# Gate folded into the output projection, input turned through DRAM, and another order in a transformer block with routed experts

## Chip, cores, metric

One core of a Trainium2 chip. The metric is the device time of one execution in microseconds, median of the runs; the profile is of one execution.

## What is computed

Sixteen sequences of 256 tokens, 256 wide, in float32. Per sequence: a layer norm with a shift from the condition, q, k and v for 16 heads of 64, a layer norm of each head's q and k, softmax attention, the output projection and the residual. Then a softmax gate over 8 experts; each expert takes its 512 best tokens, runs a two-layer network on their normalised rows, and adds the weighted result to them.

```python
h = _ln(x, ln1_g, ln1_b) + silu(t) @ W_ada.T + b_ada
q, k, v = split(h @ Wqkv.T); q, k = _ln(q), _ln(k)
o = softmax(q @ k.T / 8) @ v
x = x + o @ Wout.T
tok = x.reshape(4096, 256)
gate = softmax(tok @ Wgate.T)                  # 8 experts
vals, idx = top_k(gate.T, 512)
y = gelu(_ln(tok[idx]) @ fc1s.T + b1s) @ fc2s.T + b2s
tok = tok.at[idx].add(y * vals)
```

## The kernel before

All products are float32 on TensorE (PE), each showing as two records. A sequence `b` has two tiles `t` of 128 tokens and passes four stages.

- `First`: statistics of the input rows `xs` on VectorE (DVE), the root on GpSimd (POOL), `apply` (normalise, DVE, L632), four PE `transposes` into PSUM (`ph`, L656), and `evict` on ScalarE (ACT), which applies gain and bias and leaves `hT`, the input with its channels on the partitions (L664).
- `Group`, six column groups `g` of 512 by two tiles: the product `pm` (L693). Groups 4 and 5 are v, copied by ACT. Groups 0 to 3 are q and k: square, sum, root, scale; then they are turned. For sequence 0 (`DIRECT`) PE turns them (`pq`). For the others DVE turns blocks of 32 x 32 (`kb`, L762), a DMA writes 512 KB to DRAM (`away`, L769), and another reads them back with the blocks in place (`back`, L780); ACT's `affine` follows.
- `Quad` `d`, four heads at a time, in two halves `i`: `scores` (L819, 64 rows of the array each), `maxima` (DVE, L827), `exps` (ACT, L840), the inverse sums, `normalise` (POOL, L851). The probabilities are turned the same way: DVE (`pb`, L861), `away` (L869), `back` into `prT` (L882). The quads in `OFFS` use PE transposes (`pp`, L888) and an ACT copy (L895) instead. `product` (`po`, L907) uses 64 columns of the array each; `evict` leaves `oT`.
- `Tail`, per tile: `project` (16 records `pw` of 256 columns, L933), `residual` on DVE (`tok`), store, the second norm and its store. For the gate PE transposes `tok` (`pg`, L959), ACT copies it (`tokT`, L965), `gate` multiplies it with `wg` (`pl`, L970, in a PSUM tile of tag `po`), and DVE copies 8 columns to `gates` (L976).

When the gates of sequences 0 to 14 are there, `Routing` transposes them (`turn`, L1035) and finds each expert's threshold bit by bit: 30 rounds of a comparison on DVE, a tiny PE product (`count_over`, L1107) and a decision. Sequence 15's last quads and its projections stand between these rounds. Then 16 `Job`s follow (8 experts, two halves each): a list, a gather by GpSimd, two layers (L1293, L1309), and a scatter-add. From job 1 on the order is in plain Python.

The order up to job 0 is written out. Each step is a call `at(place, engine, took, run, needs, makes, tiles)`; `plan.order(PLACES)` sorts the steps by the numbers in the tuple `PLACES`, one for each step, and calls them; each engine then runs its instructions in that order and waits on semaphores. The other arguments of `at` are a planner's costs and act on nothing in the kernel itself:

```python
at(p, "PE", 3.47, a.project, [("oT", b)], [pw], [pw, ("oT", b)], lag=0.22)
...
for k in plan.order(PLACES):
    plan.steps[k][3]()
```

Nearly all transfers are issued by SP, in order, on one queue (q1): one that waits holds back the rest. Pools bound what can be in flight: `mm` 3 PSUM tiles (pm, ph, pw, pg), `sc` 4, `po` 1; `qk` 3, `sq` 2, `pb` 3, `prT` 4, `blocks` 4 in DRAM.

Of the kernel before, what the change touches and what calls it, by code (L numbers as in the profile page):

```python
# [9 lines left out]
F32 = mybir.dt.float32  # L10
I32 = mybir.dt.int32
BF16 = mybir.dt.bfloat16
AF = mybir.ActivationFunctionType
# [51 lines left out]
def kernel(  # L65
# [6 lines left out]
    woutT: bass.AP,  # L72
    wgateT: bass.AP,
# [75 lines left out]
    def make_others():  # L149
# [21 lines left out]
    DIRECT, OFFS = (0,), {(b, d) for b in (0, B - 1) for d in range(HP // 2)} - {(B - 1, 0), (B - 1, 1)}  # L171
# [11 lines left out]
        0, 0, 3.75, 4.52, 3.3, 4.02, 4.42, 7.76, 0.23, 0, 8, 9.39, 23.39, 15.62, 11.2, 13.11,  # L183
        20.2, 18.21, 0, 0, 0, 0, 0, 0, 0, 3.5, 4.21, 5.54, 5.02, 5.73, 6.59, 7.1, 7.76, 10.88,
        12.83, 14.5, 15.29, 17.61, 24.11, 24.82, 14.6, 16.55, 19.6, 20.39, 22.79, 26.35, 27.24,
        12.61, 14.56, 17.01, 17.93, 21.59, 25.9, 26.57, 18.4, 20.35, 22.19, 22.98, 25.11, 26.8,
        27.91, 22.38, 24.33, 29.19, 31.14, 27.46, 29.41, 30.12, 30.98, 32.96, 34.54, 35.93, 30.92,
        32.87, 33.58, 34.37, 36.58, 49.98, 53.03, 35.14, 39.48, 40.19, 43.73, 45.71, 48.98, 49.77,
        37.37, 39.98, 40.79, 41.85, 43.83, 49.5, 51.4, 39.1, 41.05, 47.25, 49.28, 32.65, 34.78,
        36.6, 38.11, 40.83, 41.54, 34.18, 34.97, 39.02, 41.27, 42.03, 37.84, 42.73, 33.67, 35.38,  # L190
        37.56, 40.03, 41.71, 42.52, 35.98, 38.52, 40.94, 42.15, 43.01, 39.76, 45.64, 46.88, 43.75,
        44.99, 45.78, 51.95, 55.85, 56.57, 46.91, 50.44, 52.86, 56.29, 57.06, 51.68, 58.63, 44.77,
        46.31, 47.37, 53.77, 61.53, 62.58, 47.51, 52.07, 54.68, 65.43, 66.15, 53.31, 66.89, 68.13,
        56.73, 58.17, 58.96, 65.08, 73.25, 73.97, 61.18, 63.07, 69.75, 75.42, 76.14, 64.31, 80.95,
        57.76, 59.98, 61.13, 63.26, 75.86, 76.63, 59.38, 60.17, 64.17, 78.03, 78.74, 62.99, 79.93,
        82.15, 65.87, 67.71, 68.62, 72.43, 89.64, 90.45, 67.11, 69.58, 71.52, 88.18, 88.9, 71.25,
        92.4, 78.91, 80.39, 81.19, 88.14, 94.44, 95.25, 84.26, 85.77, 89.05, 90.23, 94.21, 87.01,
        99.51, 101.48, 112.85, 116.83, 117.98, 117.98, 119.21, 119.72, 119.79, 120.23, 125.51,
        126.28, 116.32, 120.15, 122.66, 121.3, 122.16, 123.66, 125.96, 127.43, 132.51, 133.33, 0,
        15.1, 17.17, 27.27, 12.59, 13.3, 24.78, 46.66, 48.33, 50.66, 53.7, 54.41, 55.59, 57.57,  # L200
        58.77, 54.12, 56.07, 56.78, 59.35, 61.78, 63.16, 52.39, 54.34, 55.05, 57.47, 60.58, 62.38,
        63.18, 64.54, 67.74, 69.34, 74.46, 61.97, 64.03, 64.74, 65.99, 68.31, 69.1, 69.9, 71.34,
        74.54, 76.14, 80.34, 59.65, 62.09, 67.91, 70.54, 63.7, 65.65, 66.36, 67.87, 69.85, 70.64,
        69.79, 71.74, 72.45, 73.34, 75.32, 76.11, 71.52, 73.47, 74.18, 75.22, 77.32, 78.11, 78.91,
        80.27, 83.47, 85.07, 89.39, 73.69, 75.64, 76.72, 77.51, 79.79, 80.99, 81.79, 83.15, 86.35,
        87.95, 93.36, 76.3, 78.25, 82.84, 87.23, 81.82, 83.66, 84.81, 86.32, 87.38, 83.06, 83.85,
        87.23, 88.59, 86.05, 89.39, 90.75, 93.95, 95.55, 104.14, 88.62, 89.86, 90.94, 93.72,
        95.37, 90.46, 91.9, 94.63, 95.98, 93.34, 96.78, 98.14, 101.34, 102.94, 108.93, 114.54,
        93.42, 94.77, 95.74, 103.48, 104.54, 96.59, 101.97, 104.39, 106.35, 103.21, 107.15,
        108.51, 111.73, 113.93, 127.28, 98.49, 99.73, 100.52, 105.3, 109.36, 100.33, 102.93,  # L210
        106.21, 110.57, 104.17, 111.37, 112.73, 116.16, 118.36, 128.3, 129.49, 105.16, 107.56,
        108.71, 114.78, 117.83, 106.96, 107.75, 112.05, 116.22, 111.78, 122.3, 124.9, 128.1,
        129.97, 139.32, 106.18, 108.76, 111.12, 112.96, 114.39, 108.16, 110.16, 113.87, 115,
        112.55, 115.8, 117.16, 120.7, 122.9, 138.3, 140.41, 109.95, 112.72, 115.03, 120.22,
        125.07, 111.95, 113.58, 119.31, 129.55, 119.04, 130.35, 131.97, 135.17, 136.77, 142.08,
        121.74, 123.27, 124.06, 126.71, 130.68, 123.87, 125.02, 127.62, 128.94, 126.44, 131.48,
        133.17, 136.77, 138.77, 143.1, 145.7, 159.6, 163.6, 164.95, 164.75, 166, 166.55, 173.78,
        174.91, 176.32, 177.22, 163.07, 167.2, 168.65, 168.35, 170.41, 172.99, 176.77, 179.56,
        180.45, 181.22, 0, 26.23, 27.18, 28.97, 25.71, 26.42, 27.6, 78.47, 79.23, 84.72, 86.73,
        87.99, 89.96, 91.94, 92.73, 86.45, 88.4, 89.2, 91.84, 94.17, 97.19, 90.67, 92.86, 93.57,  # L220
        95.54, 97.8, 99, 99.8, 101.16, 104.36, 106.14, 112.08, 95.03, 96.98, 98.4, 99.19, 101.17,
        101.96, 102.94, 104.94, 108.14, 109.74, 115.99, 96.76, 103.89, 107.05, 109.67, 100.53,
        104.88, 105.75, 107.12, 109.97, 115.61, 102.41, 104.38, 105.15, 109, 111.18, 121.15,
        110.97, 113.08, 113.79, 115.69, 118.44, 119.54, 120.34, 121.7, 124.9, 126.5, 132.75,
        120.01, 121.96, 122.67, 123.46, 125.68, 126.61, 127.41, 128.77, 131.97, 134.37, 139.02,
        123.63, 126.94, 129.17, 131.31, 122.76, 127.74, 128.53, 132.16, 133.49, 124.47, 125.98,
        133.07, 134.7, 131.89, 138.37, 140.77, 143.97, 145.57, 155.83, 126.26, 128.34, 130.35,
        138.22, 139.83, 131.29, 135.85, 139.13, 140.44, 137.09, 141.24, 142.6, 145.8, 147.57,
        154.81, 156.92, 131.49, 132.73, 133.75, 136.4, 148.24, 134.1, 134.89, 137.31, 147.02,
        136.13, 149.04, 150.99, 154.95, 157.79, 171.89, 140.19, 142.03, 142.82, 145.91, 156.57,  # L230
        141.43, 143.78, 146.82, 153.56, 145.64, 157.37, 159.79, 162.99, 164.59, 172.91, 175.21,
        141.21, 143.23, 144.74, 154.31, 160.52, 145.04, 149.04, 151.52, 159.91, 150.28, 161.39,
        163.39, 167.05, 168.99, 185.54, 149.31, 150.55, 151.34, 158.04, 161.73, 154.17, 154.96,
        158.95, 162.34, 157.18, 164.59, 166.59, 169.79, 171.39, 184.52, 188.07, 150.33, 152.35,
        157.41, 160.92, 170.74, 154.77, 158.37, 160.01, 169.8, 159.74, 174.92, 177.12, 180.72,
        182.72, 190.02, 156.7, 157.94, 162.28, 165.51, 175.49, 159.14, 161.32, 166.42, 171.95,
        165.2, 176.29, 178.32, 182.68, 185.92, 191.04, 192.13, 198.43, 202.27, 204.54, 203.47,
        204.66, 207, 215.16, 215.88, 216.4, 217.76, 206.68, 210.37, 212.02, 212.16, 213.19,
        216.86, 213.06, 216.18, 222.5, 223.22, 0, 28.45, 29.46, 48.11, 26.75, 27.94, 48.44,
        131.05, 131.8, 133.11, 137.31, 138.12, 140.04, 142.63, 143.83, 134.84, 136.81, 137.52,  # L240
        141.92, 144.44, 146.41, 136.57, 138.52, 139.23, 143.8, 145.81, 147.63, 148.43, 149.79,
        152.99, 154.59, 159.33, 145.85, 147.8, 148.85, 149.64, 151.75, 152.95, 154.59, 156.59,
        159.79, 161.39, 165.59, 143.97, 146.19, 153.08, 155.92, 147.58, 150, 151.15, 152.43,
        155.97, 162.99, 151.2, 153.3, 155.37, 156.16, 158.54, 166.59, 157.72, 160.33, 161.13,
        161.92, 164.6, 165.39, 166.19, 167.79, 171.39, 173.39, 179.86, 166.54, 168.49, 169.2,
        169.99, 172.56, 173.76, 174.56, 175.92, 179.12, 180.72, 184.92, 168.27, 170.22, 174.59,
        176.65, 170, 173.16, 173.95, 178.17, 179.23, 171.35, 172.14, 179.08, 180.61, 177.71,
        182.32, 184.72, 187.92, 189.52, 195.52, 171.02, 174.37, 178.1, 180.11, 181.38, 176.1,
        177.14, 181.02, 182.59, 179.84, 184.92, 187.92, 191.12, 192.72, 212.04, 214.1, 182.63,
        185.36, 186.15, 193.17, 194.4, 184.76, 187.11, 192.26, 193.79, 190.79, 196.32, 198.54,  # L250
        205.4, 207.74, 219.75, 183.65, 190.19, 190.98, 194.08, 195.61, 187.17, 189.06, 194.99,
        196.22, 192.22, 197.02, 199.74, 202.94, 204.54, 218.73, 221.32, 196.54, 198.38, 199.53,
        202.56, 203.88, 197.78, 198.57, 201.65, 203.27, 201.38, 205.04, 206.54, 214.9, 217.74,
# [1392 lines left out]
```

## Time and profile before

| | |
|---|---|
| median of 3 runs | 1074.48 us (1072.66 to 1075.8) |
| profiled execution | 1075.44 us, its span 1073.7 us |
| busy in the span | PE 1039.4, DVE 822.4, POOL 617.5, ACT 588.9 us |
| mean granted PE clock | 0.986 |
| q1: packets, MB, share of 16 DMA engines | 156992, 235.44, 64.7% |

The span runs from the first to the last instruction. Records of PE overlap, so a row's mean length (609 ns for a pm record) is more than the distance between starts, which is what a record costs a full PE. Rows name a line, an engine, output and inputs, shape, count, busy time and mean, then the idle time before them and what ended it. Windows give each engine's busy time in a stretch, the granted clock and the share of the DMA engines.

### The profile page before, as it was taken

Reading aid. Unit: us, or ns where it says so; the run is one execution under the profiler, and the core shown is the slowest. Engines: PE = TensorE matmul, PEld = TensorE weight load, DVE = VectorE, ACT = ScalarE, POOL = GpSimd, SP = SyncE. Lnnn points to the kernel's source line nnn. Section 1 sums busy time; section 2 is a strip of 40 time slices with the busy share of each in tenths; the row PEclk is TensorE's granted clock in tenths of the full one; section 3 lists DMA queues with packets and bytes.
Section 4 is the critical chain, followed back from the end, with each engine's and each line's share of the span. In section 5 each row is a group of like instructions: output and inputs, shape, how many; then the busy total and the mean of one; then the engine's idle time right before and its main releaser. Section 6 shows DMA issues by size and latency. Waiting matters only on the chain. (4 is left out here: it accounts for less than half of the span.)

```text
span 1073.7 us, 17767 instructions
## 1 busy us (share of the span) xinstructions
PE 1039.4 (97%) x5547; PEld 681.8 (64%) x5547; DVE 822.4 (77%) x2281; ACT 588.9 (55%) x1646; POOL 617.5 (58%) x997
## 2 busy tenths in 40 slices
PE   7899999999999999999999999999789999999996
PEld 4455656555554655656565565666468888888885
DVE  6667888989888898798888888888667588655440
ACT  1577676666666666575766667675503422333331
POOL 3666776778667686766767676674401433333332
PEclk7999999999999999999999999999999999999998
DMA  6014889888987898888888898889430656665661
GB/s 217 1 60 157 279 289 319 293 294 277 309 281 262 282 317 303 294 291 271 280 296 304 280 306 282 290 315 312 147 103 21 196 146 180 196 184 155 185 204 20
DMA packets 165005, 246.85 MB, mean 230 GB/s; under 512 B 9520, under 2 KB 135728, under 8 KB 164912
## 3 DMA queue, kind: packets, MB, share of 16 engines
q1 hardware_dynamic: 156992, 235.44, 64.7%
q0 software_dynamic: 6144, 8.39, 4.3%
q10 hardware_dynamic: 1776, 1.90, 0.5%
q8 instruction: 44, 0.72, 0.3%
q14 instruction: 49, 0.40, 0.1%
HBM read 140.84 MB, written 104.86 MB: 229 GB/s over the span
## 5 line engine op out<-in xcount | busy, mean ns | idle before, releaser
L693 PE MATMUL pm<-wq,hT 128*128 128x512 f32 x768 | 362.0, 609 | 7.0 <-DVE qk L730 4.2
L851 POOL TENSOR_SCALAR pr<-pr,sums 128x256 f32<-128x256 f32 x512 | 238.2, 485 | 97.2 <-DVE sums L847 90.8
L840 ACT ACTIVATE pr<-sc,nmax 128x256 f32<-128x256 f32 x512 | 237.8, 480 | 101.5 <-DVE nmax L827 77.6
L693 PEld LDWEIGHTS pm<-wq,hT 128*128 128x128 f32 x768 | 138.2, 191 | 162.5 <-issue 137.2
L103 POOL TENSOR_TENSOR ss<-ss,neghalf 128x8 f32<-128x8 f32 x128 | 210.7, 1646 | 10.7
L827 DVE TENSOR_REDUCE nmax<-sc 128x2 f32<-128x512 f32 x256 | 165.8, 676 | 14.3 <-PE sc L819 13.6
L861 DVE STREAM_TRANSPOSE pb<-pr 128x512 f32<-128x512 f32 x232 | 154.2, 687 | 7.4 <-POOL pr L851 6.9
L819 PE MATMUL sc<-kT,qT 64*128 64x256 f32 x1024 | 135.2, 394 | 0.0
L907 PE MATMUL po<-prT,v 128*64 128x256 f32 x1024 | 128.7, 389 | 2.9 <-DMA prT<-blocks 2.9
L706 ACT ACTIVATE sq<-pm 128x512 f32<-128x512 f32 x128 | 76.7, 604 | 92.0 <-PE pm L693 91.0
L819 PEld LDWEIGHTS sc<-kT,qT 64*128 64x128 f32 x1024 | 91.3, 186 | 46.9 <-issue 28.5
L1326 POOL DMA_INDIRECT out<-y,idx x32 | 51.1, 1597 | 120.1 <-DVE y L1320 66.2
L1293 PE MATMUL ph<-xT,w 128*128 128x256 f32 x512 | 117.6, 383 | 0.0
L1309 PE MATMUL py<-w,hid 128*128 128x256 f32 x512 | 116.3, 380 | 0.0
L933 PE MATMUL pw<-wo,oT 128*128 128x256 f32 x512 | 115.2, 381 | 0.0
L907 PEld LDWEIGHTS po<-prT,v 128*64 128x64 f32 x1024 | 66.8, 137 | 68.7 <-issue 19.3
L933 PEld LDWEIGHTS pw<-wo,oT 128*128 128x128 f32 x512 | 96.3, 190 | 21.0 <-issue 5.8
L840 ACT ACTIVATION_READ_ACCUMULATOR pr<-sc,nmax 128x1 f32 x512 | 108.0, 211 | 0.0
L730 DVE TENSOR_TENSOR qk<-pm,ss 128x512 f32<-128x512 f32 x128 | 89.7, 702 | 22.8 <-POOL ss L103 20.8
L1300 ACT ACTIVATE hid<-ph,vec 128x256 f32<-128x256 f32 x128 | 60.4, 474 | 84.2 <-PE ph L1293 77.2
L1309 PEld LDWEIGHTS py<-w,hid 128*128 128x128 f32 x512 | 95.6, 190 | 12.8
L1293 PEld LDWEIGHTS ph<-xT,w 128*128 128x128 f32 x512 | 95.5, 190 | 12.9
(142 smaller groups left out, 1081.6 us busy)
## 6 DMA issues: line engine op xcount, KB each, us to landing
blocks<-pb SPq DMA_DIRECT2D x116, 512.0 KB
prT<-blocks SPq DMA_DIRECT2D x116, 512.0 KB
kblocks<-kb SPq DMA_DIRECT2D x60, 512.0 KB
w<-in_fc2T SPq DMA_DIRECT2D x16, 1024.0 KB
w<-in_fc1T SPq DMA_DIRECT2D x16, 1024.0 KB
qraw<-kblocks SPq DMA_DIRECT2D x30, 512.0 KB
kT<-kblocks SPq DMA_DIRECT2D x30, 512.0 KB
out<-tok SPq DMA_DIRECT2D x32, 128.0 KB
```

The costliest lines, as they stand in the source:

```text
L103: nc.gpsimd.tensor_tensor(dst, src, neghalf[:, : src.shape[1]], ALU.pow)
L693: nc.tensor.matmul(self.pm, hTs[self.b][:, c, bass.ts(self.t, P)], wq[:, c, bass.ts(self.g, GW)], start=(c == 0), stop=(c == DC - 1),)
L730: engine.tensor_tensor(dst, src.rearrange("p (q e d) -> p q e d", q=QB, e=8), by_head(self.ss[:, 1, :]), ALU.mult,)
L819: nc.tensor.matmul(self.sc[i, j][:, t, :], qTs[self.b][rows, hp, bass.ts(t, P)], keys[rows, hp] if whole else keys[rows, hp // 4, hp % 4], ...
L827: nc.vector.tensor_reduce(self.nmax[i, j], self.sc[i, j], AX.X, ALU.max, negate=True)
L840: nc.scalar.activation(dst, src, AF.Exp, bias=self.nmax[i, j][:, t : t + 1], scale=1.0, accum_out=self.sums[i][:, 0, j, t : t + 1],)
L851: nc.gpsimd.tensor_scalar(self.pr[i, j][:, t, :], self.pr[i, j][:, t, :], self.sums[i][:, 1, j, t : t + 1], 1.0, ALU.mult, ALU.mult,)
L861: nc.vector.transpose(self.pb[i][:, :, :, j].rearrange("p k c t n -> p t k c n"), self.pr[i, j].rearrange("p t (k c m) -> p t k c m", c=TB ...
L907: nc.tensor.matmul(self.po[j * HD : (j + 1) * HD, i, :], vs[self.b][:, c, bass.ts(4 * self.d + 2 * i + j, HD)], prT[:, j, c] if (self.b, s ...
L933: nc.tensor.matmul(self.pw, oTs[self.b][:, hp // 2, self.t, hp % 2, :], wo[:, hp, :], start=(hp == 0), stop=(hp == HP - 1),)
L1293: nc.tensor.matmul(self.ph[f], self.w1[:, c, bass.ts(f, P)], self.xT[:, c, :], start=(c == 0), stop=(c == DC - 1),)
L1309: nc.tensor.matmul(self.py[i], self.hid[:, f, bass.ts(i, P)], self.w2[:, f, :], start=(f == 0), stop=(f == FC - 1),)
```

## The change

- `wo` gets 8 more columns per head pair: Wout transposed times the gate matrix, computed once by `Fold` from a second load of Wout (1 MB). `project` then yields the attention's share of the gate's logits beside the projection; two more products add the share of the input, from `xT`, the input transposed on the host and loaded for each sequence (256 KB). The transposes of `tok`, the copy and the gate's own step go.
- The normalised input of sequences 1 to 15 is turned by DVE and through DRAM (`xblocks`, 256 KB out in 2-KB rows and back in 512-byte pieces), no longer by PE; `apply` moves to GpSimd for them. The buffers are of the tags `qk` and `sq`. Weights and vectors are permuted on the host to match (`quarters`).
- Quads 2 and 3 of sequence 0 leave `OFFS`: they go through DRAM, too.
- `PLACES` is another list, with other costs in the `at` calls.

```diff
-    ... {(B - 1, 0), (B - 1, 1)}
+    ... {(B - 1, 0), (B - 1, 1), (0, 2), (0, 3)}
+    XDIRECT = (0,)
-    PLACES = (0, 0, 3.75, 4.52, 3.3, ...)
+    PLACES = (...)
-        wo = attw.tile([P, HP, D], F32, name="wo")
+        wo = attw.tile([P, HP, D + E], F32, name="wo")
+        def load_xT(b):
+            xTs[b] = seq.tile([P, DC, N], F32, tag="xT", bufs=1, name=f"xT{b}")
+            nc.sync.dma_start(xTs[b], xT[:, b * N : (b + 1) * N].rearrange("(c p) n -> p c n", p=P))
+        class Fold:
+            def load(self):
+                self.w = seq.tile([P, DC, H * HD], F32, tag="oT", bufs=2, name="wout")
+                nc.sync.dma_start(self.w, wout.rearrange("(c p) f -> p c f", p=P))
+            def product(self):
+                self.pf = ps.tile([P, HP, E], F32, tag="mm", bufs=3, name="pf")
+                for hp in range(HP):
+                    for c in range(DC):
+                        nc.tensor.matmul(self.pf[:, hp], self.w[:, c, bass.ts(hp, P)], wg[:, c],
+                            start=(c == 0), stop=(c == DC - 1))
+            def evict(self):
+                nc.scalar.copy(wo[:, :, D:], self.pf)
 class First:
+                self.norms[t].apply(dst, nc.vector if self.b in XDIRECT else nc.gpsimd)
+            def turn(self, t):
+                if t == 0:
+                    self.xb = work.tile([P, QB, DC, TB, SQ], F32, tag="qk", bufs=3, name="xb")
+                nc.vector.transpose(...)
+            def away(self):
+                self.blocks = dram.tile([QB, SQ, QB, P], F32, tag="xblocks", bufs=2, name="xblocks")
+                nc.sync.dma_start(...)
+            def back(self):
+                self.raw = work.tile([P, QB, DC, TB, SQ], F32, tag="sq", bufs=2, name="xraw")
+                nc.sync.dma_start(...)
+            def affine(self):
+                for c in range(DC):
+                    nc.scalar.activation(hTs[b][:, c]..., self.raw[:, :, c], AF.Identity, bias=..., scale=...)
 class Tail:
-            def project(self, a=0, b=HP):
+            def project(self):
+                self.pw = ps.tile([P, D + E], F32, tag="mm", bufs=3, name="pw")
                 for hp in range(HP):
                     nc.tensor.matmul(self.pw, oTs[...], wo[:, hp, :], start=(hp == 0), stop=False)
+                for c in range(DC):
+                    nc.tensor.matmul(self.pw[:, D:], xTs[self.b][:, c, bass.ts(self.t, P)], wg[:, c, :],
+                        start=False, stop=(c == DC - 1))
-            def transposes(self): ...
-            def evict(self): ...
-            def gate(self): ...
             def gate_evict(self):
-                nc.vector.tensor_copy(gates[:, self.n, :], self.pl)
+                nc.vector.tensor_copy(gates[:, self.n, :], self.pw[:, D:])
```

## The prediction

> **What bounds the kernel now.** I read the page first (busy shares, slices, queues), then the windows by stage, the order of time on PE around one sequence's end, the waits of PE, and the order of time where the sequences give way to the routing.
>
> From the page: PE is busy nearly throughout, and the DMA slices are the only others near nine.
>
> ```profile
> PE 1039.4 (97%) x5547; PEld 681.8 (64%) x5547; DVE 822.4 (77%) x2281; ACT 588.9 (55%) x1646; POOL 617.5 (58%) x997
> ...
> DMA  6014889888987898888888898889430656665661
> ...
> q1 hardware_dynamic: 156992, 235.44, 64.7%
> ```
>
> The windows (stretch, length, busy time of each engine, granted clock, DMA share, GB/s) split it into stages.
>
> ```profile
> 60.00:100.00 40.00, 40.00 (x187) 21.55 (x187) 28.32 (x50) 30.02 (x81) 28.97 (x46) 1.00 0.34 119
> 100.00:750.00 650.00, 649.62 (x3186) 375.20 (x3183) 562.65 (x1123) 432.59 (x1279) 460.73 (x796) 1.00 0.86 291
> 750.00:821.00 71.00, 58.03 (x441) 44.99 (x440) 51.74 (x261) 21.29 (x63) 17.60 (x37) 0.93 0.32 105
> 821.00:1074.00 253.00, 242.85 (x1548) 212.60 (x1546) 141.39 (x767) 78.43 (x161) 82.15 (x67) 0.99 0.55 156
> ```
>
> From 60 to 750 us PE never rests, so each sequence takes as long as its PE work. The projections of sequences 0 and 13 begin at 120.28 and 717.76, which is 46.0 us a sequence. DVE is at 87% there, POOL at 71%, DMA at 86%. From 750 to 821 the routing's chain between DVE and PE sets the time; from 821 the experts run, which the change doesn't touch. So the question is when the routing's first transpose (L1035) can run.
>
> The order of time on PE (start, length, line, records) gives prices as distances between starts:
>
> ```profile
> 177.61 2.00 PE L819 MATMUL sc<-kT,qT 64*128 64x256 f32 x16
> 179.54 1.95 PE L907 MATMUL po<-prT,v 128*64 128x256 f32 x16
> 181.42 0.44 PE L959 MATMUL pg<-ident,tok 128*128 128x128 f32 x2
> 181.69 0.60 PE L656 MATMUL ph<-ident,xn 128*128 128x128 f32 x4
> 182.13 1.88 PE L693 MATMUL pm<-wq,hT 128*128 128x512 f32 x4
> 183.85 0.51 PE L970 MATMUL pl<-wg,tokT 128*128 128x8 f32 x4
> 184.21 0.42 PE L959 MATMUL pg<-ident,tok 128*128 128x128 f32 x2
> 184.47 3.60 PE L693 MATMUL pm<-wq,hT 128*128 128x512 f32 x8
> ```
>
> The four transposes of the input cost 0.44 us (181.69 to 182.13), the two of tok 0.27 and 0.26, the gate's four records 0.36. Ahead of another full-array product four pm records take 1.72 (182.13 to 183.85); ahead of scores they took 1.81 (175.80 to 177.61), so a change between whole array, half rows (scores) and half columns (products) costs 0.09.
>
> **The change, part by part, to the routing's transpose.** Counts are from PE's order in the two programs, up to that transpose.
> - Input transposes of sequences 1 to 15 go: 15 x 0.44 = -6.6.
> - The tok transposes of 30 tiles go: 30 x 0.26 = -7.8.
> - The gate's two products per tile become two of xT with the same gate weights: 30 x 0.36 out, the same in, 0.
> - The projection gets 264 columns for 256. Its 32 records of sequence 14 run from 743.63 to 750.74, 0.222 each; 8/256 of that, 16 records, 30 tiles: +3.3.
> - The fold is 16 products of the gate's kind (two in 0.36): +2.9. It stands in the head, where PE idles (16.69 of 20 us busy from 20 to 40), so it may cost nothing; I count it.
> - Quads 2 and 3 of sequence 0 go through DRAM, while two of sequence 15's transposing steps move ahead of the routing: 64 transposes become 40, 24 x 0.11 (0.44/4) = -2.6.
> - One more half-quad product stands ahead: +0.9 (1.88 for two).
> - The other order changes array shape 286 times, where the old one did 258: 28 x 0.09 = +2.5. The diff doesn't say this; it takes back a sixth of what the transposes give.
>
> The sum is -6.6 - 7.8 + 3.3 + 2.9 - 2.6 + 0.9 + 2.5 = **-7.4 us** of PE work.
>
> The Trainium skill (TensorEngine Tiling, Key Properties) says that changing the tiling mode drains TensorE, and gives no time. The 0.09 us above is that price here; without it the sum would read -9.9.
>
> Beside the path: DVE loses 30 applies (0.43 each, -13.0) and gains 30 turns of 128x256 (between 0.34, half of L861's 0.69, and 0.69; I take 0.38, +11.4) and 8 turns of sequence 0 (+5.5): 4 us more on an engine with 87 us free in the stage. ACT loses the tokT copies and 8 prT copies (-12.2 - 4.8) and keeps the affine at its size. The applies go to POOL, 30 x 0.485 as L851's: +14.6, ahead of normalisations that wait there; POOL has 189 us free. SP issues some 55 more transfers of 0.3 to 0.5 us. Its new waits matter more: each `back` of the input waits for its write, as L882 does (95.3 us over 53 waits, 1.8 each), and behind it stand the writes of other quads. That is hidden as long as the products come later than their data. The input's own exchange is well covered: between its affine and the first product that reads hT stand three to eleven steps of PE, 3.5 us or more.
>
> DMA is the cover that wears thin. Per sequence three transfers of 0.262 MB come in (input out, input back, xT); 291 GB/s x 46.0 is 13.4 MB now. PE's new period is about 45.5, so 14.2 MB in it is 311 GB/s, a share of 0.86 x 311/291 = 0.92. By packets the input's read is worse: 512 of 512 bytes, which at q1's mean packet (64.7% of 16 x 1073.7 us over 156992, 0.071 us) would take 2.3 us of all engines against 0.8 by bytes. So the share lies between 0.92 and 0.95.
>
> The Trainium skill (DMA: Bandwidth & Descriptors, Bandwidth) puts HBM per core at about 358 GB/s. By that alone there would be 13% left; this trace shows no 650-us stage near it, only 291.
>
> What a late transfer costs shows where DMA is fullest:
>
> ```profile
> PE po L907 <- DMA prT<-blocks: 2.9, 3, 1.1
> ```
> ```profile
> 743.63 7.17 PE L933 MATMUL pw<-wo,oT 128*128 128x256 f32 x32
> ...
> 757.05 1.13 PE L819 MATMUL sc<-kT,qT 64*128 64x256 f32 x8
> ...
> 759.17 1.08 PE L907 MATMUL po<-prT,v 128*64 128x256 f32 x8 [0.98 <-DMA prT<-blocks]
> ...
> 760.18 0.50 PE L1035 MATMUL pgT<-ident,gate_of 128*128 128x128 f32 x2
> ```
>
> All three waits of the trace, 0.95 us each, lie at 759 to 765, after the experts' first weights were queued; one is ahead of the routing's transpose. In the sequence stage there is none. At 0.92 and over I don't expect none: I take three more, +2.9, with bounds of none (0) and one per sequence (14 x 0.95 = 13.3).
>
> After the transpose, the old loop holds both projections of sequence 15, tok's transposes and the gate; the new one has one projection inside and one behind, ahead of the totals. DVE's decisions now wait up to 2.7 us for PE (790.55), once per projection; so it may save 2.7 us or, if the totals wait longer than the round did, cost 1 (PE's 3.7 for a projection less 2.7). I take 0.
>
> So -7.4 + 2.9 = **-4.5 us**. The profiled execution took 1075.44 (span 1073.7 and 1.7 around it) and becomes 1070.9; it was 0.96 over the median of 1074.48, so the median becomes **1070.0**.
>
> **Rivals.**
> 1. *DMA becomes the bound (slower).* Products wait for prT in the sequence stage. One 0.95 us wait per sequence gives -7.4 + 13.3 = +5.9, 1080.4. Eight waits eat the saving; from eleven on it is slower by over 0.3%. For it: 5-us windows from 705 to 750 already show shares of 0.96 to 1.07. Against it: PE rode over them without a wait.
> 2. *The gain is lost at the end (no change).* Ahead of the routing's transpose now stand three products of sequence 15 instead of two, with an expert's 2.2 MB of weights queued before their reads. Three waits more there, with the three above: -7.4 + 2.9 + 2.9 = -1.6, 1072.9.
> 3. *No waits, and a shorter loop (much faster).* -7.4 - 2.7 = -10.1, 1064.4.
>
> **How the numbers follow.** A run of this kernel tells about 0.3% (3.2 us) from no change: faster means under 1071.3, slower over 1077.7. The forecast with its neighbourhood (1066.5 to 1071.3) gets 0.46, rival 3 gets 0.08, rival 2 0.22, rival 1 0.24. Faster 0.54, same 0.22, slower 0.24. The range runs from 1064.0, rival 3, to 1081.0, just past rival 1's price; below it lies 0.05, above it 0.15.
>
> **What would show it.** Right: PE still busy in all of 100 to 750, the projections of sequences 0 and 13 about 45.5 us a sequence apart, no ph rows but sequence 0's, DMA share 0.91 to 0.95, the routing's transpose near 755. Wrong: more than eight waits of PE or its weight loads for prT, qT or kT; a DMA share of 0.97 and up with PE under 640 of 650; or the transpose early but the experts' first product not (then the loop took it). A head that ends later, by the fold or by late keys of sequence 1, would move the first projection past 120.

## The result, and the profile after

| | before | after |
|---|---|---|
| median of 4 runs | 1073.57 us (1071.77 to 1075.8) | 1087.53 us (1084.88 to 1088.7) |
| profiled execution, span | 1075.44, 1073.7 | 1088.7, 1087.0 |
| routing's first transpose on PE | 760.18 | 772.65 |
| from there to the experts' first product | 60.51 | 61.18 |

The ratio of the means is 1.0126 (95%: 1.0097 to 1.0154). The forecast was 1070.0, the range 1064.0 to 1081.0: the change made the kernel slower, by more than any case that I had priced. All but 0.7 of the 13.3 us between the profiled executions lie ahead of the routing's transpose.

The page of the kernel after (busy times; slices; the SP queue):

```profile
PE 1039.5 (96%) x5423; PEld 670.9 (62%) x5423; DVE 822.0 (76%) x2289; ACT 575.8 (53%) x1607; POOL 654.5 (60%) x1027
...
DMA  7028899998899998989898799899403556655661
...
q1 hardware_dynamic: 174384, 252.74, 68.5%
```

The windows of the kernel after, the second cut at the same places as before, the third up to the experts' first product:

```profile
100.00:750.00 650.00, 641.27 (x3038) 356.01 (x3037) 555.39 (x1119) 422.56 (x1245) 485.01 (x810) 1.00 0.90 307
750.00:834.00 84.00, 66.75 (x476) 51.49 (x477) 57.38 (x270) 22.89 (x69) 22.99 (x49) 0.89 0.35 120
```

PE does 124 records fewer in all and is no less busy; in the sequence stage it now rests 8.7 us of 650, where it rested 0.4. The DMA share of that stage is 0.90, under the 0.92 to 0.95 that I gave. POOL is busy 37 us more in all, where I had 14.6. Two rows of GpSimd after show why:

```profile
L927 POOL TENSOR_SCALAR pr<-pr,sums 128x256 f32<-128x256 f32 x512 | 237.4, 485 | 93.4 <-DVE sums L923 82.8 <-PE pm L769 2.6
...
L672 POOL TENSOR_SCALAR xn<-xs,mv,rs 128x256 f32<-128x256 f32 x30 | 37.1, 1241 | 0.9
```

The apply has the shape of the normalisation that I took its price from, and takes 1.241 us for 0.485. What that does shows in the waits of ACT and DVE from 100 to 745 us (total, times, longest), first before, then after:

```profile
ACT pr L840 <- DVE nmax L827: 70.7, 51, 4.6
...
DVE qk L730 <- POOL ss L103: 13.3, 27, 1.4
```
```profile
ACT pr L916 <- DVE nmax L903: 94.4, 60, 4.7
...
DVE qk L806 <- POOL ss L105: 28.2, 32, 2.5
```

And one such place in the order of time after:

```profile
422.32 2.43 POOL L672 TENSOR_SCALAR xn<-xs,mv,rs 128x256 f32<-128x256 f32 x2
...
425.12 1.67 POOL L105 TENSOR_TENSOR ss<-ss,neghalf 128x8 f32<-128x8 f32 x1
...
426.82 0.69 DVE L806 TENSOR_TENSOR qk<-pm,ss 128x512 f32<-128x512 f32 x1 [2.49 <-POOL ss L105]
...
427.56 1.98 PE L769 MATMUL pm<-wq,hT 128*128 128x512 f32 x4 [0.76 <-DVE qk L806]
...
428.02 2.47 DVE L903 TENSOR_REDUCE nmax<-sc 128x2 f32<-128x512 f32 x4
...
429.39 0.47 ACT L916 ACTIVATE pr<-sc,nmax 128x256 f32<-128x256 f32 x1 [1.92 <-DVE nmax L903]
...
431.23 1.10 PE L769 MATMUL pm<-wq,hT 128*128 128x512 f32 x2 [1.69 <-DVE qk L806]
```

Two applies hold the root of q and k's norm back; DVE stands 2.49 us for it, with the maxima behind in its order; ACT stands for the maxima; PE stands twice for `qk`, whose PSUM tile it needs.

The end of the sequences, PE after:

```profile
744.19 1.64 PE L895 MATMUL sc<-kT,qT 64*128 64x256 f32 x10
747.93 1.94 PE L895 MATMUL sc<-kT,qT 64*128 64x256 f32 x6 [2.10 <-DVE pb L937]
750.88 2.08 PE L895 MATMUL sc<-kT,qT 64*128 64x256 f32 x8 [1.01 <-ACT kT L870]
752.89 2.93 PE L983 MATMUL po<-prT,v 128*64 128x256 f32 x16
...
769.56 1.08 PE L983 MATMUL po<-prT,v 128*64 128x256 f32 x8 [1.56 <-DMA prT<-blocks]
```

There is nothing but sequence 15's own chain to do at 746 to 751, and after the waits the granted clock falls: 0.81 from 745 to 750, 0.51 from 750 to 755, and eight score records take 2.08 us for 1.13. The Trainium skill (TensorE: Matmul & The Clock Gate, Part 1) says that the clock goes to half rate after an idle window of about 3.4 us. The 0.51 agrees with the half; the idle time does not, since PE's longest rest here was 2.10 us.

**PE's time up to the routing's transpose**, counted from the starts of its records: *work* is records times their usual distance to the next (medians: pm 0.429, pw 0.216 or, with 264 columns, 0.222, a transpose 0.109, scores 0.1085, products 0.108, fold 0.112, and the gate's four in 0.364); *changes* are what a stretch of one array shape takes on top of that (0.199 for the whole array, 0.104 on its first pm record and 0.094 on its last; 0.196 for scores, 0.150 for products); *rest* is what remains, split at 60 and 700 us. Each row is of one profiled execution, and executions of one kernel differ by up to 7 us (f3: 1074.09 to 1081.1), so differences of a microsecond say little.

| kernel | transpose at | work | changes | rest | head, sequences, end |
|---|---|---|---|---|---|
| before | 760.2 | 688.5 | 47.7 | 24.0 | 20.7, 1.8, 1.5 |
| after | 772.7 | 680.1 | 52.5 | 40.0 | 22.0, 9.4, 8.6 |
| e1, applies on DVE | 767.3 | 680.1 | 52.5 | 34.7 | 20.8, 5.6, 8.3 |
| h1, cheap apply on GpSimd | 767.2 | 680.1 | 52.5 | 34.6 | 20.8, 5.6, 8.1 |
| f4, e1 and the tail moved | 766.7 | 680.1 | 52.9 | 33.6 | 19.7, 5.3, 8.6 |
| g1, f4 and weights later | 763.8 | 680.1 | 52.9 | 30.7 | 21.5, 6.1, 3.2 |
| h3, g1 and xT loaded once | 760.0 | 680.1 | 52.9 | 26.9 | 19.4, 4.4, 3.1 |
| e5, before with the slow apply on GpSimd | 772.2 | 688.5 | 47.7 | 36.0 | 23.7, 10.4, 1.8 |
| h4, before with the cheap apply there | 766.6 | 688.5 | 47.7 | 30.4 | 23.6, 5.3, 1.4 |
| f3, before with spare traffic | 762.0 | 688.5 | 47.7 | 25.8 | 18.8, 3.9, 3.2 |
| g2, before with the fold | 768.8 | 688.4 | 46.5 | 33.9 | 19.6, 9.3, 5.0 |

The change does take PE's time off, 8.37 of work less 4.83 of changes, 3.5 us; the rest grows by 16.0.

### The profile page after: what moved, and what is told of

It is laid out like the page before. It is cut to its first block, busy times and chain, and to the rows that moved or that the text cites. A ratio compares the mean times of both kernels' runs of the same rounds, so it can differ in the third digit from the quotient of the medians.

```text
span 1087.0 us, 17596 instructions
## 1 busy us (share of the span) xinstructions
PE 1039.5 (96%) x5423; PEld 670.9 (62%) x5423; DVE 822.0 (76%) x2289; ACT 575.8 (53%) x1607; POOL 654.5 (60%) x1027
## 5 line engine op out<-in xcount | busy, mean ns | idle before, releaser
L903 DVE TENSOR_REDUCE nmax<-sc 128x2 f32<-128x512 f32 x256 | 164.3, 673 | 16.9 <-PE sc L895 16.5
L937 DVE STREAM_TRANSPOSE pb<-pr 128x512 f32<-128x512 f32 x240 | 157.9, 684 | 9.9 <-POOL pr L927 7.7
L895 PE MATMUL sc<-kT,qT 64*128 64x256 f32 x1024 | 138.3, 399 | 4.1 <-DVE pb L937 2.1
L983 PE MATMUL po<-prT,v 128*64 128x256 f32 x1024 | 132.8, 392 | 3.8 <-DMA prT<-blocks 3.3
L1008 PE MATMUL pw<-wo,oT 128*128 128x264 f32 x512 | 122.4, 393 | 0.0
L786 DVE TENSOR_REDUCE ss<-sq 128x8 f32<-128x512 f32 x128 | 85.4, 668 | 25.2 <-ACT sq L782 24.3
```

Source lines behind the costliest of these rows:

```text
L895: nc.tensor.matmul(self.sc[i, j][:, t, :], qTs[self.b][rows, hp, bass.ts(t, P)], keys[rows, hp] if whole else keys[rows, hp // 4, hp % 4], ...
L903: nc.vector.tensor_reduce(self.nmax[i, j], self.sc[i, j], AX.X, ALU.max, negate=True)
L937: nc.vector.transpose(self.pb[i][:, :, :, j].rearrange("p k c t n -> p t k c n"), self.pr[i, j].rearrange("p t (k c m) -> p t k c m", c=TB ...
L983: nc.tensor.matmul(self.po[j * HD : (j + 1) * HD, i, :], vs[self.b][:, c, bass.ts(4 * self.d + 2 * i + j, HD)], prT[:, j, c] if (self.b, s ...
L1008: nc.tensor.matmul(self.pw, oTs[self.b][:, hp // 2, self.t, hp % 2, :], wo[:, hp, :], start=(hp == 0), stop=False,)
```

## Experiments: the applies

Three theories. 1: the applies on GpSimd hold back the chain root, scale, maxima, exponentials, PE. 2: the fuller DMA delays data. 3: the order itself, with its end stage. Ratios are to the kernel before, run beside each.

**e1**, the changed kernel with the applies on DVE:

```diff
-                self.norms[t].apply(dst, nc.vector if self.b in XDIRECT else nc.gpsimd)
+                self.norms[t].apply(dst, nc.vector)
```

> The changed kernel with one thing undone: the normalisation of the input (xn) of sequences 1 to 15 is applied by DVE, as in the kernel before, not by GpSimd; everything else, the exchange and the order included, as changed. Theory 1 (the 30 applies on GpSimd, 1.24 us each, hold back the roots behind them, and through DVE, the maxima and the exponentials PE): 7 to 10 us less than the changed kernel, 1077 to 1080, idle of DVE for the root's result back from 28 to about 14 us in the sequence stage, routing's transpose at 763 to 766. Theory 2 (the fuller DMA) and theory 3 (the other order itself, with its end stage): within 2 us of the changed kernel, 1086 to 1089.

1081.15 us, ratio 1.0062 (1.0048 to 1.0076): half of the loss, a little less than theory 1 had. DVE's wait for the root went down less than expected:

```profile
DVE qk L806 <- POOL ss L105: 21.5, 29, 2.1
```

**e5**, the kernel before with only the applies moved to GpSimd:

```diff
...
-                self.norms[t].apply(self.xn[t])
+                self.norms[t].apply(self.xn[t], nc.gpsimd if self.b else nc.vector)
```

> The kernel before with one thing of the change alone: the normalisation of the input of sequences 1 to 15 is applied by GpSimd in the old order, nothing else. Theory 1: 30 applies of 1.24 us on GpSimd, 3 to 12 us slower than before, 1077 to 1086, with more idle of DVE for the root's result (13.3 us before in the sequence stage). Theory 2 and theory 3: no change, within 2 us of 1074.

1088.45 us, 1.0137 (1.0122 to 1.0152). In an order that was laid for them on DVE the 30 instructions alone lose as much as the whole change does.

**f1**, the changed kernel, each apply as two instructions:

```diff
...
+                    nc.gpsimd.tensor_scalar(dst, norm.src, norm.mv[:, 0:1], None, ALU.subtract)
+                    nc.gpsimd.tensor_scalar(dst, dst, norm.rs[:, 1:2], None, ALU.mult)
```

> The changed kernel with each apply on GpSimd written as two instructions, a subtraction with one pointer and a multiplication with one pointer, for the one instruction with both that took 1.24 us. If the 1.24 us comes from having two operations in one instruction, each of the two costs about 0.48 as the multiplication of the probabilities does, 0.97 together, GpSimd loses 8 us and theory 1 expects 1 to 3 us less than the changed kernel (the gain of putting the applies back on DVE, 6.4 us for 37 us of GpSimd, in proportion). If each of the two costs 0.6 or more, the price is of the data and not of the form, and the time stays within 1 us or grows. Theories 2 and 3: no change.

A miss: 1102.55 us, 1.0271 (1.0252 to 1.029). Each of the two costs nearly twice what I took:

```profile
L698 POOL TENSOR_SCALAR xn<-xn,rs 128x256 f32<-128x256 f32 x30 | 28.3, 945 | 2.8
L697 POOL TENSOR_SCALAR xn<-xs,mv 128x256 f32<-128x256 f32 x30 | 28.0, 933 | 0.0
```

The same multiplication by a pointer takes 0.479 us at the probabilities, where the code adds a second operation, times 1.0. So the form was at stake, and **g4** looked at five forms by turns (the sequence's number modulo 5 chooses):

```diff
...
+                if form == 0:
+                    ts(dst, src, mu, rs, ALU.subtract, ALU.mult)
+                elif form == 1:
+                    ts(dst, src, rs, nm, ALU.mult, ALU.add)
+                elif form == 2:
+                    ts(dst, src, mu, 1.0, ALU.subtract, ALU.mult)
+                    ts(dst, dst, rs, 1.0, ALU.mult, ALU.mult)
+                elif form == 3:
+                    ts(dst, src, nm, rs, ALU.add, ALU.mult)
+                else:
+                    ts(dst, src, rs, 1.0, ALU.mult, ALU.mult)
+                    ts(dst, dst, nm, 1.0, ALU.add, ALU.mult)
```

> A look at the price of forms: the changed kernel, its apply on GpSimd written in five ways by turns over the sequences, all of which compute the same. (a) subtract pointer, multiply by pointer in one instruction: 1.24 us as measured. (b) multiply by pointer, add pointer: 1.24 if the price is that of two pointers. (c) subtract pointer, times the constant 1.0; then multiply by pointer, times the constant 1.0: 2 x 0.48 if the price is that of the second pointer, 2 x 0.93 if only multiplications are cheap. (d) add pointer, multiply by pointer: as (b). (e) multiply by pointer, times 1.0; add pointer, times 1.0: 0.48 and 0.48 or 0.93. The probabilities' normalisation (multiply by pointer, times the constant 1.0) took 0.48, the single operation with no second one 0.93.

Its rows (1084.93 us, one run):

```profile
L704 POOL TENSOR_SCALAR xn<-xs,mv,rs 128x256 f32<-128x256 f32 x6 | 7.3, 1219 | 0.4
L708 POOL TENSOR_SCALAR xn<-xs,mv 128x256 f32<-128x256 f32 x6 | 6.9, 1148 | 0.2
...
L706 POOL TENSOR_SCALAR xn<-xs,rs,nm 128x256 f32<-128x256 f32 x6 | 3.3, 555 | 0.6
L711 POOL TENSOR_SCALAR xn<-xs,nm,rs 128x256 f32<-128x256 f32 x6 | 3.3, 548 | 0.7
...
L713 POOL TENSOR_SCALAR xn<-xs,rs 128x256 f32<-128x256 f32 x6 | 2.9, 478 | 0.0
L714 POOL TENSOR_SCALAR xn<-xn,nm 128x256 f32<-128x256 f32 x6 | 2.9, 478 | 0.6
```

Neither the second pointer nor addition is dear (0.555, 0.548, 0.478): the subtraction is (1.219, 1.148). Adding the negated mean does the same for less than half.

**h1**, the changed kernel with that form (**h4**: the same in the kernel before):

```diff
...
+                nc.gpsimd.tensor_scalar(nm, norm.mv[:, 0:1], -1.0, 1.0, ALU.mult, ALU.mult)
+                nc.gpsimd.tensor_scalar(dst, norm.src, nm, norm.rs[:, 1:2], ALU.add, ALU.mult)
```

> The changed kernel with one thing changed: the apply on GpSimd adds the negated mean and then multiplies, for subtracting the mean and multiplying (0.55 us in place of 1.22, and a GpSimd instruction of 128x1 of 0.19 for the sign): 22 us of GpSimd for 37. If the loss goes with GpSimd's time, 6.4 x 15/37 = 2.6 us less than the changed kernel, 1084 to 1085.5. If it is the long instruction that holds back the roots behind it, most of the 6.4 us comes back: 1081 to 1083. If the place itself matters (any apply on GpSimd), under 1 us.

1081.89 us, 1.0062 (1.0049 to 1.0074), the ratio of e1. The two waits of the chain fall with it: ACT's for the maxima from 94.4 to 78.8 us, DVE's for the root from 28.2 to 22.1. Together: 0 us of applies on GpSimd give 1.0062, 22.6 us in short instructions 1.0062, 37 us in 1.24-us ones 1.0126, 56 us in pairs of 0.94 1.0271. Within the intervals of e1 and h1, some 1.4 us to each side, the form is all of theory 1's loss in this order, and the place costs nothing.

> The kernel before with the applies of sequences 1 to 15 on GpSimd in the cheap form, old order. The slow form cost 14 us there. In proportion to GpSimd's time (22 of 37 us): 8 us slower, 1081 to 1084. If the long instruction was the trouble: 0 to 4 us slower, 1074 to 1079.

1081.40 us, 1.0049 (1.0036 to 1.0062) for 1.0137: in between. In the old order the place costs something, too; of its 6.4 us more rest 2.9 are in the head, where sequence 1's applies join GpSimd's queue.

## Experiments: the traffic

**e4**, the changed kernel with `xT` loaded once, and **h3**, the same on g1 (below):

```diff
+            if b:
+                xTs[b] = xTs[0]
+                return
             xTs[b] = seq.tile([P, DC, N], F32, tag="xT", bufs=1, name=f"xT{b}")
```

> The changed kernel with the transposed input loaded once, for sequence 0, and used for all 16 sequences (the gate's logits are then of another input: that part of the computation is changed). It takes 15 of the 45 new transfers of 0.26 MB and their issues on SP away. Theory 2: 2 to 4 us less than the changed kernel. Theory 1: 1 us less at most. Theory 3: 0 to 1 us less, through the freer SP queue in the end stage.

1084.15 us, 1.0095 (1.008 to 1.011); 3.4 us less than the changed kernel by the medians, 0.0031 less in the ratio, though the intervals overlap a little.

**f3**, the kernel before with 42 spare transfers:

```diff
...
+                if aways[self.b] in (2, 5, 7):
+                    spare = dram.tile([N, D], F32, tag="spare", bufs=4, name="spare")
+                    nc.sync.dma_start(spare, x[self.b * N : (self.b + 1) * N])
```

> The kernel before, old order, no part of the change, with three spare transfers of 0.26 MB (rows of the input to a scratch buffer in DRAM, read by nobody) issued by SP in each of sequences 1 to 14, 42 in all, 11 MB: the change's own additional traffic without its steps. Theory 2: 3 to 8 us slower than before (the changed kernel lost 3.4 us less with a third of its traffic taken away). Theories 1 and 3: within 1.5 us of 1074.

1077.01 us, 1.0026 (1.0013 to 1.004): 2.7 us, just under theory 2's range.

> The kernel with the moved tail and the weights later (1078.5), with the transposed input loaded once and used for all sequences (the gate's logits are then of another input: that part of the computation is changed). Theory 2: a third of the additional traffic less gives 1.5 to 3 us, 1075.5 to 1077, as 3.4 were gained by the same edit on the changed kernel and 2.7 lost by 11 MB of spare traffic on the kernel before. If that gain was GpSimd's or the end stage's, now gone: within 1 us of 1078.5.

1076.47 us, 1.0008 (0.9999 to 1.0018) for g1's 1.0037: 3 us again, with GpSimd and the end stage out of the way. So loading `xT` for every sequence costs about 3 us. PE itself waits for no transfer in the sequence stage; ACT and DVE do. From 100 to 745 us their waits for transfers come to 4.1 us before, 9.8 after, 16.9 in g1 and 9.1 in h3 (one execution each).

Whether the bytes or SP's queue carry it isn't told apart, since loading `xT` once takes both away. One thing speaks for the queue. `xT` has a single buffer, so SP stands until the projections of the sequence before have read it, 21.2 us in 13 waits of the changed kernel from 100 to 745 us, and whatever comes next on the queue stands behind it, here a read of prT:

```profile
SPq L573 <- PE pw L1013: 21.2, 13, 3.7
```
```profile
406.00 0.37 SPq L958 DMA_DIRECT2D prT<-blocks  x1
410.09 0.38 SPq L573 DMA_DIRECT2D xT<-in_xT  x1
410.57 0.42 SPq L958 DMA_DIRECT2D prT<-blocks  x1
```

The spare transfers of f3 show no such wait, and 11 MB of them cost no more than the 4 MB of `xT`. A second buffer for `xT` was not tried.

## Experiments: the end stage

**f4**, e1 with sequence 13's second projection, its followers and the load of `xT` 14 moved into the idle time:

```diff
+        MOVED = {
+            3278: 721.2, 3279: 727.9, 3286: 727.95, ...
+            3284: 730.2, 3285: 732, 3502: 725.6, ...
+        }
-        for k in plan.order(PLACES):
+        for k in plan.order([MOVED.get(k, p) for k, p in enumerate(PLACES)]):
```

> The changed kernel with the applies back on DVE and one more edit: the second projection of sequence 13, with its followers and the load of sequence 14's transposed input, is moved from among sequence 15's last matrix products to the place where PE idles between the scores of sequence 15 (2.1 and 1.8 us of waits, and 2.5 us more at a lower granted clock after them). Theory 3 (the order of the end stage leaves PE without independent work there): 3 to 6 us less than 1081.2, that is 1075 to 1078. If the idle time comes from a chain that just starts later (transfers, exponentials), nothing is gained: 1080 to 1082.

1080.59 us, 1.006 (1.0046 to 1.0073): no gain. The projections of sequence 14 began at 746.1 for 752.5, but PE lost it all at the next transfer (order of time of PE, then of SP's issues):

```profile
756.14 1.13 PE L895 MATMUL sc<-kT,qT 64*128 64x256 f32 x8
761.21 1.97 PE L983 MATMUL po<-prT,v 128*64 128x256 f32 x8 [3.93 <-DMA prT<-blocks]
```
```profile
747.73 0.44 SPq L1268 DMA_DIRECT2D w<-in_fc2T  x1
748.26 0.89 SPq L1270 DMA_DIRECT2D w<-in_fc1T  x1
...
749.85 3.00 SPq L945 DMA_DIRECT2D blocks<-pb  x2
752.90 6.01 SPq L958 DMA_DIRECT2D prT<-blocks  x2
```

An expert's 2.1 MB of weights stand ahead of the write, and the read's issue waits for that write, 6 us for two.

**g1** is f4 with that load moved behind sequence 15's reads:

```diff
...
+            3916: 743.0,
...
```

> The kernel with the applies on DVE and the moved tail of sequence 13 (1080.6), with one more edit: the first load of an expert's weights (2.1 MB) is issued behind the last reads of sequence 15's probabilities, not ahead of them. In the version before it PE lost its two waits of 2.1 and 1.8 us, but then stood 3.93 us (and 1.5 more at a lower clock) for prT behind those weights. If the weights on the queue are what makes that read late (rival 2 of the prediction): 4 to 5.5 us less, 1075 to 1077, no wait of PE for prT over 1 us ahead of the routing's transpose. If the read is late by its own chain (turns, write, wait of SP): within 1.5 us of 1080.6.

1078.53 us, 1.0037 (1.0023 to 1.0051): 2 us by medians, half of what I expected, but the mechanism is there: the wait is 0.58, the clock 1.00 from 740 to 764, the end's rest 3.2 for 8.6.

```profile
760.46 1.08 PE L983 MATMUL po<-prT,v 128*64 128x256 f32 x8 [0.58 <-DMA prT<-blocks]
```

The Trainium skill (DMA: Bandwidth & Descriptors, Queues, rings and completion order) says that each DMA engine consumes a queue's descriptors in ring order; the waits of 3.93 us with the weights ahead and 0.58 with them behind agree with it.

**g3** and **h2** are g1 with the applies on ACT, by `activation(..., bias=norm.nm, scale=norm.rs[:, 1:2])`, and on GpSimd in the cheap form.

> As the kernel with the weights issued later, and the applies of sequences 1 to 15 on ACT (one activation with scale and bias by pointer), 5 us later in the order, with a small GpSimd instruction of 128x1 for each bias. ACT is busy 65% in the sequence stage, DVE 88%, GpSimd 71%. Theory 1 in its wider form (what counts is how long the engine that takes the applies delays the chain from root to maxima to exponentials): DVE gets 12 us back, 1 to 4 us less than the kernel with the weights later. If the exponentials are the chain's tight step, ACT's 30 x 0.4 us more make it 1 to 5 us slower.

> The kernel with the moved tail and the weights later (1078.5, applies on DVE), with the applies back on GpSimd in the cheap form. GpSimd gets 22 us, DVE loses 12.6. If GpSimd's order is the tight one (theory 1): 1 to 4 us slower, 1079.5 to 1082.5. If a cheap apply on GpSimd is as good as one on DVE or better, as the prediction took it (0.485 each, hidden): 1076 to 1079.

1077.82 us, 1.0027 (1.0016 to 1.0037), and 1080.03 us, 1.0038 (1.0023 to 1.0053), for g1's 1.0037. Once none of them is slow, which engine takes the applies is hardly seen.

## Experiments: the fold alone

**e2**, **f5** and **g2** keep the old order and its transposes of the input, and only fold the gate:

```diff
-        wo = attw.tile([P, HP, D], F32, name="wo")
+        wo = attw.tile([P, HP, D + E], F32, name="wo")
...
+                for c in range(DC):
+                    nc.tensor.matmul(
+                        self.pw[:, D:], xTs[self.b][:, c, bass.ts(self.t, P)], wg[:, c, :],
+                        start=False, stop=(c == DC - 1),
+                    )
```

> The kernel before, in its old order, with the first part of the change alone: the gate matrix folded into the output projection (264 columns, two products of the untouched input per tile), no transposes of the tokens, no exchange of the input. By the sum on record this part takes 7.8 us of PE work off and puts 3.3 + 2.9 on, so 2 us less than before (up to 5 where the fold lies in PE's idle time of the head): 1069 to 1072. Theory 1 and theory 3 expect that (GpSimd's work and the order are those of before); theory 2 expects 0 to +3 from 5 MB more of DMA.

1098.52 us, 1.0227 (1.0214 to 1.024), slower than the whole change. The waits of PE name two late loads that I had placed badly:

```profile
PE pw L977 <- DMA xT<-in_xT: 7.5, 1, 7.5
PE pm L723 <- ACT hT L694: 6.5, 1, 6.5
```

> The kernel before, old order, with the fold alone as before, but its loads out of the head (behind the first exchange of sequence 1), its product later in sequence 0, and the last transposed input loaded a sequence ahead. It takes away the two waits that made the first version lose 24 us: input tiles behind the fold's weights (first matrix product of the normalised input at 17.5 us for 10.8) and 7.5 us for the last transposed input. By my sum on record the fold is worth 2 us (7.8 less 3.3 and 2.9, with 2.9 hidden or not): 1069 to 1073. If the longer projection makes DVE wait in its order (20 us of waits for the projection, 7.7 before), the saving is lost and the time stays at 1074 to 1080.

1092.67 us, 1.018 (1.0162 to 1.0198). The head was mended; the wait for `xT` was still there, 7.86 us, because it was sequence 14's and I had moved sequence 15's.

> The fold alone in the old order, with the last late load mended: the transposed input of sequence 14 is loaded at once behind sequence 13's last projection. In the version before it PE waited 7.86 us for it, with about 2 us more at a lower clock. So 9 to 11 us less than 1092.7: 1081 to 1084. What then remains over the kernel before (7 to 10 us) is no late load: the work of PE counted by its starts is the same (691.0 us with the fold and without), and its idle time in the sequence stage is 7 us more. If it comes down to 1074 or less, the whole loss was late loads.

1086.07 us, 1.011 (1.0096 to 1.0124). With neither late load left the fold alone costs 11.5 us by medians. PE's work is the same with it and without, 688.4 and 688.5 us (the expectation's 691.0 counts the gate's records at 0.112 each): 60 tok transposes of 0.109 less, 6.5, against 480 projection records of 0.006 more, 2.9, and the fold's 32 of 0.112, 3.6. And DVE, whose next step is the residual, waits for a projection that ends later (before, then g2, from 100 to 745):

```profile
DVE tok L940 <- PE pw L933: 7.7, 12, 1.5
```
```profile
DVE tok L994 <- PE pw L981: 20.0, 24, 1.9
```

These 12 us of DVE are the largest difference that I found; that they make the 7.5 us more rest in the sequence stage is argued, not shown. The edit also moves DVE's copy to `gates` up, directly behind the residual, which no run took back. An order made for the fold, as the changed kernel has, doesn't show them (2.5 us in 3 waits there).

## Why the prediction was wrong, step by step

- **The applies on POOL** are the step that failed first: "30 x 0.485 as L851's: +14.6, ahead of normalisations that wait there; POOL has 189 us free". The nearest row had the same operation, engine and shape, but another pair of operations, and I gave no upper bound. It measured 30 x 1.241 = 37.1 us, and it was not hidden: with the form alone changed (h1) the ratio goes from 1.0126 to 1.0062, about 7 us. The second half of the sentence was wrong in kind: 189 us free over a stage say nothing about 2.4 us in front of one root.
- **PE's sum**, -7.4, measured -3.5. The terms without changes of shape were -9.9 and came out as -8.4 (tok's transposes 0.22 a tile for 0.26, the fold 3.6 for 2.9). The changes were mis-sized: 0.09 is only what the last record of a whole-array stretch takes more. Its first takes 0.104 more, as 533 ns for 429 show, and stretches of scores and products take 0.196 and 0.150, so the 28 further changes cost 4.8 for 2.5. The fold, which "may cost nothing", is in the 680.1; its 32 records last 5.64 us in the head, but the head's rest grew by only 1.3.
- **The assumption under the sum**, that saved work is saved time as long as PE never rests, holds only where the others keep up. The fold alone shows it: work the same, rest up by 9.9.
- **DMA**, +2.9 as three waits of PE for prT in the sequence stage, had the size by luck and not the mechanism: no such wait came there. `xT` costs 3 us all the same, and ACT and DVE are the ones that wait for transfers. Share 0.90 for 0.92 to 0.95: packets of 512 bytes took 28 ns on average, so the input's read costs 0.9 us of all engines, near the lower bound of 0.8.
- **Rival 2**, the end, named the right place and a part of the mechanism: "three products of sequence 15 instead of two, with an expert's 2.2 MB of weights queued before their reads". It was priced at +2.9 from waits of 0.95; the end's rest grew by 7.1. In the changed kernel the wait for prT ahead of the transpose is 1.56; the larger part is 2.10 and 1.01 us within sequence 15's own chain, where PE had no independent work, and half clock after them. With the tail moved the weights show in full, 3.93 us (f4).
- **Rival 1**, DMA as the bound, is out: it needs some twelve waits for prT in the sequence stage. Its price came nearest the result by luck.
- **After the transpose**, 0: measured +0.67 (61.18 less 60.51). Right in size.
- The sum of what the traces show: -3.5 + 16.0 + 0.7 = 13.2; the profiled executions differ by 13.26.

Of the rest's 16.0 us the form of the applies makes 5.4 (after to h1), the order of the end with the weights 3.9 (h1 to g1), the loads of `xT` 3.8 (g1 to h3), each from single profiled executions. By the ratios the same steps are 6.9, 2.7 and 3.1 us. The 2.9 that remain stay open; 2.6 of them stand in the sequence stage, and the exchange of the input and the other order of that stage are the candidates that no run took away.

No version came out under the kernel before. The best that computes everything, g3, stands at 1.0027 (1.0016 to 1.0037); with `xT` loaded once h3 can't be told from the kernel before (1.0008, 0.9999 to 1.0018).

## What to carry to other kernels

Price a moved instruction by a row with the same operations, not only the same engine and shape; where there is none, bound it by the dearest row of that engine, and ask what is next in its queue, not how idle it is. A saving on a saturated engine counts only after its new order has been laid; look at the end of the stage for work that no longer covers a chain. Keep bulk loads behind the last small transfers that somebody waits for, and ask what a load into a single buffer holds back on an ordered queue.

## What the runs showed of the hardware

- GpSimd, 128x256 in float32: multiply then multiply, or add then multiply by a constant, 0.48 us; addition and multiplication with two pointers 0.55; one operation alone 0.93 to 0.95; subtraction and then multiplication 1.15 to 1.24 (f1, g4 and the changed kernel).
- PE: at full clock a stretch of one array shape takes more than its records' usual distances, 0.199 us for the whole array (pm: 533 ns for 429 on the first record, 523 on the last), 0.196 for half rows (scores) and 0.150 for half columns (products) (before and after, 100 to 700 us).
- DMA: packets of 512 bytes took 28 ns, of 1 KB 52, of 2 KB 97, of 4 KB 170 on average from 100 to 745 us of the changed kernel, so the smallest are a third dearer by the byte than the largest.
